# One projection product over the whole array, and row 0's uniform attention through one block and a row sum

## The chip, the cores and the metric

The kernel runs on one core of one Trainium2 chip, in fp32 throughout. The metric is the device time of the program in microseconds. The engines are named as in the profile: PE is TensorE's matmul stream and PEld its weight loads, DVE is VectorE, ACT is ScalarE, POOL is GpSimd, and SP is the engine that issues most of the plain DMAs.

## The reference

Eight sequences of 512 tokens with 256 features go through three residual steps:

```
x = x + 0.5 * moe(layernorm(x))          # f1
x = x + attention(layernorm(x))
x = x + 0.5 * moe(layernorm(x))          # f2

attention(x):                            # x: 8 x 512 x 256, already normalised
    sim   = x x^T / 16                   # only s < t counts
    A     = the 8 best s for each t (fewer where t < 8, none for t = 0)
    q, k  = x Wq^T, x Wk^T               # 32 features each
    score = q k^T / sqrt(32), and -1e9 where A is 0
    msg   = softmax(score) x
    return gelu(gain * (mix * x + (1 - mix) * msg) + bias) * scale
```

Row 0 of a sequence has no earlier token, so all its 512 scores are -1e9 and its softmax is uniform: its message is the mean over all 512 rows. Every other row has at least one chosen neighbour, and its weights outside the chosen ones are zero. The expert step (moe) sends each token to two of eight experts with 512 hidden features.

## The kernel before, in words

The tokens of a whole step are sorted into **tiles** of 256 slots, each for one expert. There are 39 tiles for f1, then 13 for f2 over the first five sequences (f2a) and 26 for the rest (f2b). A loop over all 78 tiles writes out the order of every engine's instructions by hand; nothing is reordered after that. For each tile it emits four times `up` (eight passes of 128x256 into `ph`, a silu on ACT, a product `g` on DVE), the transposes of the next tile's rows (`ptx`, copied to `xT` by DVE), two times `down` (eight passes each into `py`), and two times `put`: ACT scales `py` to `y`, and POOL issues an indirect DMA that adds the rows to `acc_d`. Between the two `put`s POOL issues the gather of a later tile's weights (`w`), after them the gathers of its rows (`xr`). fp32 products run as two passes per matmul instruction, transposes as one.

Between these pieces the loop calls `side()`, which advances a generator by one step: the attention of one sequence after another, and, where it is due, the routing of f2a and f2b. A sequence starts two tiles after its rows are complete, so that one sequence of attention falls into every four tiles of f1. Each engine works its instructions off in the order in which they were emitted; whatever waits holds up what is behind it on that engine.

One sequence of attention has these steps, a `side()` call each:

- layernorm on DVE (`xn`), then on POOL two operations over the whole sequence for `own`, the part of the output that doesn't depend on the neighbours;
- the transposes of `xn` into `xnT`;
- the queries, then the keys: a product of `wq_sb` and of `wk_sb` (128x32 each) with `xnT`, both into tiles called `pq`, copied by ACT into `q` and `k_`, 32 partitions each. In the loop the first stands between the two `down`s of a tile, the second after its `put`s;
- nine steps in which the four blocks c of 128 rows pass through a chain, one step apart: `similar` (`psim` on PE, `sim` on ACT, the mask of the diagonal block on POOL), `choose` (MAX8 and MATCH_REPLACE on DVE), `score` (`psc` on PE with 32 rows of the array, then `kept`, `hit`, `sc`, `nmax` on DVE), `exponential` (ACT), `turn` (transposes `pte` on PE, `exT` on DVE), `message` (`pm` on PE, `msg` and the sum into `own` on DVE). Block c works on columns 0 to (c+1)*128.

Block 0 holds row 0. In `exponential`, `turn` and `message` it is therefore worked over all 512 columns; the columns from 128 on are a constant -1e9, written once into two buffers `first`. Within a step the order is choose, exponential, message, turn, score, similar, each for its block.

All PSUM tiles of the attention and the routing come from one pool of three buffers in turn (`ps_a`), so a new product waits until the third product before it has been read. `ph` has three buffers of its own; `sim`, `hit`, `ex` and `exT` have two each in SBUF.

```
L573            for n, wn in enumerate((wq_sb, wk_sb)):
L576                    pq[:DH, :T], lhsT=wn[:, k, :], rhs=xnT[:, k, :], start=(k == 0), stop=(k == KD - 1)
L621            nc.tensor.matmul(psc[:, :W], lhsT=q[:, c * P : W], rhs=k_[:, :W], start=True, stop=True)
L642            W = T if c == 0 else (c + 1) * P
L671        for j in range(NC + len(steps) - 1):
L672            for lag in (1, 3, 5, 4, 2, 0):
```

Of the kernel before, what the change touches and what calls it, by code (L numbers as in the profile page):

```python
# [9 lines left out]
F32 = mybir.dt.float32  # L10
I32 = mybir.dt.int32
U32 = mybir.dt.uint32
AF = mybir.ActivationFunctionType
ALU = mybir.AluOpType
# [4 lines left out]
P = 128  # L19
# [7 lines left out]
def kernel(  # L27
# [13 lines left out]
    nc = tc.nc  # L41
    B, T, D = x.shape
    DH = wqT.shape[1]
    E = gwT.shape[1]
    KD = D // P
    FF = wexp.shape[1] // (3 * KD)
    KF = FF // P
    NC = T // P
# [17 lines left out]
    const = ctx.enter_context(tc.tile_pool(name="const", bufs=1))  # L66
    dram = ctx.enter_context(tc.tile_pool(name="dram", bufs=1, space=DRAM))
    wpool = ctx.enter_context(tc.tile_pool(name="wpool", bufs=3))
    work = ctx.enter_context(tc.tile_pool(name="work", bufs=2))
# [6 lines left out]
    ps_a = ctx.enter_context(tc.tile_pool(name="ps_a", bufs=3, space=PSUM))  # L76
# [34 lines left out]

    gw_sb = const.tile([P, KD, E], F32, tag="gw_sb", name="gw_sb")
    nc.scalar.dma_start(gw_sb, gwT.rearrange("(k p) e -> p k e", p=P))
    wq_sb = const.tile([P, KD, DH], F32, tag="wq_sb", name="wq_sb")
    nc.scalar.dma_start(wq_sb, wqT.rearrange("(k p) h -> p k h", p=P))
    wk_sb = const.tile([P, KD, DH], F32, tag="wk_sb", name="wk_sb")
    nc.scalar.dma_start(wk_sb, wkT.rearrange("(k p) h -> p k h", p=P))
    gain_sb = const.tile([P, D], F32, tag="gain_sb", name="gain_sb")
    nc.scalar.dma_start(gain_sb, gain.to_broadcast([P, D]))
    bias_sb = const.tile([P, D], F32, tag="bias_sb", name="bias_sb")  # L120
# [20 lines left out]
    scale = const.tile([P, 1], F32, tag="scale", name="scale")  # L141
# [3 lines left out]

    first = []
    for i in range(2):
        t = const.tile([P, T], F32, tag=f"first{i}", name=f"first{i}")
        nc.vector.memset(t[:, P:], MASKED)
        first.append(t)  # L150


    def layernorm(src, name):
# [28 lines left out]
    def transposed(xn, name):  # L182

        xnT = work.tile([P, KD, T], F32, tag="xnT", name=f"xnT_{name}")
        for k in range(KD):
            pt = ps_a.tile([P, 512], F32, tag="pa", name=f"pt_{name}_{k}")
            for c in range(NC):
                nc.tensor.transpose(pt[:, c * P : (c + 1) * P], xn[:, c, k * P : (k + 1) * P], ident)  # L188
            nc.scalar.copy(xnT[:, k, :], pt[:, :T])
        return xnT  # L190
# [369 lines left out]
    def attention(b, x1, tables):  # L560

        xn = yield from layernorm(x1, f"at_{b}")

        own = work.tile([P, NC, D], F32, tag="own", name=f"own_{b}")
        nc.gpsimd.tensor_mul(own, xn, mix_gain.unsqueeze(1).to_broadcast([P, NC, D]))
        nc.gpsimd.tensor_add(own, own, bias_sb.unsqueeze(1).to_broadcast([P, NC, D]))
        yield
        yield
        xnT = transposed(xn, f"at_{b}")
        yield  # L570
        qk = []
        for n, wn in enumerate((wq_sb, wk_sb)):
            pq = ps_a.tile([P, 512], F32, tag="pa", name=f"pq{n}_{b}")  # L573
            for k in range(KD):
                nc.tensor.matmul(  # L575
                    pq[:DH, :T], lhsT=wn[:, k, :], rhs=xnT[:, k, :], start=(k == 0), stop=(k == KD - 1)  # L576
                )
            t = work.tile([DH, T], F32, tag=f"qk{n}", name=f"qk{n}_{b}")
            nc.scalar.activation(t, pq[:DH, :T], AF.Copy, scale=1.0 / math.sqrt(DH) if n == 0 else 1.0)
            qk.append(t)  # L580
            yield
        q, k_ = qk
        sims, hits, scores, exs, exTs = {}, {}, {}, {}, {}

        def similar(c):

            W = (c + 1) * P
            rows = slice(c * P, W)
            psim = ps_a.tile([P, 512], F32, tag="pa", name=f"psim_{b}_{c}")
            for k in range(KD):  # L590
                nc.tensor.matmul(  # L591
                    psim[:, :W], lhsT=xnT[:, k, rows], rhs=xnT[:, k, :W], start=(k == 0), stop=(k == KD - 1)
                )
            sim = work.tile([P, T], F32, tag="sim", name=f"sim_{b}_{c}")
            nc.scalar.activation(sim[:, :W], psim[:, :W], AF.Copy, scale=1.0 / math.sqrt(D))
            nc.gpsimd.affine_select(
                out=sim[:, rows], in_=sim[:, rows], pattern=[[-1, P]], compare_op=ALU.is_gt, fill=NEG, base=0,
                channel_multiplier=1,
            )
            sims[c] = sim  # L600

        def choose(c):

            W, sim = (c + 1) * P, sims[c]
            top = small.tile([P, 8], F32, tag="top", name=f"top_{b}_{c}")
            nc.vector.max(top, sim[:, :W])
            hit = work.tile([P, T], F32, tag="hit", name=f"hit_{b}_{c}")
            nc.vector.match_replace(hit[:, :W], top, sim[:, :W], HIT)
            if c == 0:

                nc.gpsimd.affine_select(
                    out=hit[:, :P], in_=hit[:, :P], pattern=[[-1, P]], compare_op=ALU.is_gt, fill=0.0, base=0,
                    channel_multiplier=1,
                )
            hits[c] = hit

        def score(c):

            W, hit = (c + 1) * P, hits[c]
            psc = ps_a.tile([P, 512], F32, tag="pa", name=f"psc_{b}_{c}")  # L620
            nc.tensor.matmul(psc[:, :W], lhsT=q[:, c * P : W], rhs=k_[:, :W], start=True, stop=True)  # L621
            kept = work.tile([P, T], F32, tag="kept", name=f"kept_{b}_{c}")
            nc.vector.scalar_tensor_tensor(
                kept[:, :W], hit[:, :W], HIT, psc[:, :W], ALU.is_equal, ALU.mult
            )
            nc.vector.tensor_scalar(hit[:, :W], hit[:, :W], HIT, MASKED, ALU.is_lt, ALU.mult)
            sc = first[b % 2] if c == 0 else work.tile([P, W], F32, tag=f"sc{c}", name=f"sc_{b}_{c}")
            nc.vector.tensor_add(sc[:, :W], kept[:, :W], hit[:, :W])
            nmax = small.tile([P, 1], F32, tag=f"nmax{c}", name=f"nmax_{b}_{c}")
            nc.vector.tensor_reduce(nmax, sc[:, :W], AX.X, ALU.max, negate=True)  # L630
            scores[c] = sc, nmax

        def exponential(c):
            W = T if c == 0 else (c + 1) * P
            sc, nmax = scores[c]
            ex = work.tile([P, T], F32, tag="ex", name=f"ex_{b}_{c}")
            tot = small.tile([P, 1], F32, tag=f"tot{c}", name=f"tot_{b}_{c}")
            nc.scalar.activation(ex[:, :W], sc[:, :W], AF.Exp, bias=nmax, accum_out=tot)
            exs[c] = ex, tot

        def turn(c):
            W = T if c == 0 else (c + 1) * P  # L642
            pt = ps_a.tile([P, 512], F32, tag="pa", name=f"pte_{b}_{c}")
            for s in range(W // P):
                nc.tensor.transpose(pt[:, s * P : (s + 1) * P], exs[c][0][:, s * P : (s + 1) * P], ident)
            exT = work.tile([P, T], F32, tag="exT", name=f"exT_{b}_{c}")
            nc.vector.tensor_scalar(exT[:, :W], pt[:, :W], 0.0, None, ALU.max)
            exTs[c] = exT

        def message(c):  # L650
            W = T if c == 0 else (c + 1) * P
            pm = ps_a.tile([P, 512], F32, tag="pa", name=f"pm_{b}_{c}")
            for s in range(W // P):
                nc.tensor.matmul(  # L654
                    pm[:, :D],
                    lhsT=exTs[c][:, s * P : (s + 1) * P],
                    rhs=xn[:, s, :],
                    start=(s == 0),
                    stop=(s == W // P - 1),
                )  # L660

            part = small.tile([P, 1], F32, tag="part", name=f"part_{b}_{c}")
            nc.vector.reciprocal(part, exs[c][1])
            nc.vector.tensor_scalar(part, part, 0.0, rest, ALU.max, ALU.mult)
            msg = work.tile([P, D], F32, tag="msg", name=f"msg_{b}_{c}")
            nc.vector.scalar_tensor_tensor(msg, pm[:, :D], part, gain_sb, ALU.mult, ALU.mult)
            nc.vector.tensor_add(own[:, c, :], own[:, c, :], msg)


        steps = (similar, choose, score, exponential, turn, message)  # L670
        for j in range(NC + len(steps) - 1):  # L671
            for lag in (1, 3, 5, 4, 2, 0):  # L672
                if 0 <= j - lag < NC:
                    steps[lag](j - lag)
            yield

        nc.scalar.activation(own, own, AF.Gelu)
        yield
        nc.vector.scalar_tensor_tensor(x1, own, scale, x1, ALU.mult, ALU.add)
        yield  # L680
        yield from ffn_begin(b, x1, "f2", tables)
# [161 lines left out]
```

## Time and profile before

| | |
|---|---|
| time, three runs | 1261.3 us median (1258.34, 1261.3, 1262.29) |
| the profiled execution | 1258.32 us; span 1256.6 us, TensorE clock 0.98 |
| PE, PEld busy | 1159.4 us, 955.8 us |
| DVE, ACT, POOL busy | 573.7 us, 343.6 us, 532.8 us |
| DMA | 195.30 MB, 155 GB/s |
| pq matmuls (L575) | 64 passes of 128x512, 592 ns median each |
| psc matmuls (L621) | 64 passes, 270 to 692 ns |
| POOL on own (L565, L566) | 8 x 2355 ns and 8 x 2345 ns |

[...] passes that follow each other start closer together than their durations. The start-to-start distance is therefore what a group costs on PE. A number in brackets behind a row of the trace is the idle time of that engine ahead of the instruction and what ended it. The span runs roughly like this: set-up and routing of f1 until 116 us, expert tiles alone until about 260, attention between the tiles until 840, the routing of f2b beside tiles of f2a until 945, and tiles alone to the end.

### The profile page before, as it was taken

The page shows a single profiled execution, that of the slowest core. Times are in us where ns is not written, and L with a number is a line of the kernel's source. Part 1 is how long each engine was busy: PE and PEld are TensorE (multiplying, and loading weights), DVE is VectorE, ACT ScalarE, POOL GpSimd, SP SyncE. Part 2 cuts the span into 40 slices and gives each one's busy share as a digit, 9 for nine tenths or more (in the row PEclk, how much of TensorE's full clock was granted, in tenths as well). Part 3 has the DMA queues.
Part 4 walks back from the last instruction along what each step waited for, and adds up shares of the span by engine and source line. Part 5 has one row for each costly group of instructions (what it writes and reads, how often), then busy time and mean ns, then how long its engine had stood idle before and what let it go on. Part 6 is the DMA issues. An engine that isn't in the chain of part 4 may idle for free.

```text
span 1256.6 us, 14941 instructions
## 1 busy us (share of the span) xinstructions
PE 1159.4 (92%) x5470; PEld 955.8 (76%) x5470; DVE 573.7 (46%) x1713; ACT 343.6 (27%) x718; POOL 532.8 (42%) x464
## 2 busy tenths in 40 slices
PE   5854999989999999999799999998999999999996
PEld 4743888867768676777668778687888888888885
DVE  7484221226555564736768465567732222221221
ACT  2200122224343343424323243342122222222221
POOL 0002355553443435352522544534345555554553
PEclk9997999989999999999999999999999999999998
DMA  8402566654645346363622645344456776677664
GB/s 296 150 1 112 183 182 182 188 155 129 184 114 152 121 137 181 86 197 103 184 68 67 185 134 175 91 154 134 135 138 197 201 201 187 183 215 233 190 198 91
DMA packets 69337, 195.30 MB, mean 155 GB/s; under 512 B 8336, under 2 KB 54160, under 8 KB 59152
## 3 DMA queue, kind: packets, MB, share of 16 engines
q0 software_dynamic: 41184, 163.60, 45.3%
q1 hardware_dynamic: 25600, 29.36, 7.0%
q10 hardware_dynamic: 2480, 1.39, 0.4%
q8 instruction: 43, 0.70, 0.2%
q14 instruction: 30, 0.25, 0.1%
HBM read 156.05 MB, written 42.47 MB: 158 GB/s over the span
## 4 chain that ended last, share of the span: by engine, by line
PE 63%; DVE 15%; issue 11%; DMA 4%; ACT 4%; POOL 1%; POOLq 0%; ACTq 0%; DVEq 0%
PE ph_f L522 14%; PE ph_f2b L522 11%; PE py_f L537 9%; PE py_f2b L537 6%; PE ph_f2a L522 4%; PE py_f2a L537 3%; PE psim L591 3%; PE pm L654 2%; PE pq L575 2%; DMA acc_d_f<-y_f2b,tokens_f2b 2%; DMA xr_f2b<-xn_d_f,tokens_f2b 1%; PE psc L621 1%; PE pt_at L188 1%; PE pg_f L217 1%; PE pl_f2b L369 1%
## 5 line engine op out<-in xcount | busy, mean ns | idle before, releaser
L522 PE MATMUL ph_f<-xT_f,w_f 128*128 128x256 f32 x1248 | 289.0, 384 | 0.8 <-DVE xT_f L514 0.8
L522 PEld LDWEIGHTS ph_f<-xT_f,w_f 128*128 128x128 f32 x1248 | 235.7, 192 | 44.7 <-issue 11.2
L549 POOL DMA_INDIRECT acc_d_f<-y_f,tokens_f x78 | 125.5, 1609 | 261.8 <-ACT y_f L548 223.5
L522 PE MATMUL ph_f2b<-xT_f2b,w_f2b 128*128 128x256 f32 x832 | 183.8, 379 | 0.0
L531 DVE TENSOR_TENSOR g_f<-silu_f,ph_f 128x256 f32<-128x256 f32 x156 | 64.3, 418 | 258.9 <-ACT silu_f L530 257.0
L522 PEld LDWEIGHTS ph_f2b<-xT_f2b,w_f2b 128*128 128x128 f32 x832 | 158.1, 190 | 21.5
L537 PE MATMUL py_f<-w_f,g_f 128*128 128x256 f32 x624 | 148.8, 389 | 0.0
L531 DVE TENSOR_TENSOR g_f2b<-silu_f2b,ph_f2b 128x256 f32<-128x256 f32 x104 | 43.8, 421 | 223.8 <-ACT silu_f2b L530 223.8
L537 PEld LDWEIGHTS py_f<-w_f,g_f 128*128 128x128 f32 x624 | 117.1, 194 | 27.1 <-issue 13.0
L549 POOL DMA_INDIRECT acc_d_f<-y_f2b,tokens_f2b x52 | 83.2, 1601 | 109.3 <-DMA acc_d_f<-y_f2b,tokens_f2b 56.0
L530 ACT ACTIVATE silu_f<-ph_f 128x256 f32<-128x256 f32 x156 | 59.7, 383 | 224.6 <-PE ph_f L522 209.8
L537 PE MATMUL py_f2b<-w_f2b,g_f2b 128*128 128x256 f32 x416 | 95.6, 383 | 0.0
L522 PE MATMUL ph_f2a<-xT_f2a,w_f2a 128*128 128x256 f32 x416 | 95.1, 380 | 0.0
L479 POOL DMA_INDIRECT w_f<-in_wexp,wrow_f x39 | 38.5, 987 | 123.2 <-DVE wrow_f L475 111.6
L479 POOL DMA_INDIRECT xr_f<-xn_d_f,tokens_f x78 | 76.6, 982 | 23.8 <-issue 23.8
L522 PEld LDWEIGHTS ph_f2a<-xT_f2a,w_f2a 128*128 128x128 f32 x416 | 77.7, 190 | 11.6 <-issue 1.6
L537 PEld LDWEIGHTS py_f2b<-w_f2b,g_f2b 128*128 128x128 f32 x416 | 78.2, 193 | 9.9
L549 POOL DMA_INDIRECT acc_d_f<-y_f2a,tokens_f2a x26 | 41.9, 1613 | 93.0 <-ACT y_f2a L548 89.1
L530 ACT ACTIVATE silu_f2b<-ph_f2b 128x256 f32<-128x256 f32 x104 | 39.9, 383 | 127.8 <-PE ph_f2b L522 126.5
L548 ACT ACTIVATE y_f<-py_f,wslot_f 128x256 f32<-128x256 f32 x78 | 32.7, 470 | 103.4 <-PE py_f L537 103.4
L479 POOL DMA_INDIRECT xr_f2b<-xn_d_f,tokens_f2b x52 | 50.4, 968 | 15.8 <-issue 15.8
L531 DVE TENSOR_TENSOR g_f2a<-silu_f2a,ph_f2a 128x256 f32<-128x256 f32 x52 | 21.5, 418 | 72.3 <-ACT silu_f2a L530 72.2
(349 smaller groups left out, 1545.5 us busy)
## 6 DMA issues: line engine op xcount, KB each, us to landing
xn_d_f<-xn_f SPq DMA_DIRECT2D x16, 512.0 KB
xin<-in_x SPq DMA_DIRECT2D x8, 512.0 KB
acc_d_f<-xin SPq DMA_DIRECT2D x8, 512.0 KB
x<-acc_d_f SPq DMA_DIRECT2D x8, 512.0 KB
acc_d_f<-x SPq DMA_DIRECT2D x8, 512.0 KB
out<-acc_d_f SPq DMA_DIRECT2D x8, 512.0 KB
xr_f<-xn_d_f,tokens_f POOLq DMA_INDIRECT x78
acc_d_f<-y_f,tokens_f POOLq DMA_INDIRECT x78
```

The costliest lines, as they stand in the source:

```text
L188: nc.tensor.transpose(pt[:, c * P : (c + 1) * P], xn[:, c, k * P : (k + 1) * P], ident)
L217: nc.tensor.matmul(pg[:, c, :], lhsT=xnT[:, k, c * P : (c + 1) * P], rhs=gw_sb[:, k, :], start=(k == 0), stop=(k == KD - 1),)
L479: nc.gpsimd.indirect_dma_start(out=dst, out_offset=None, in_=table, in_offset=bass.IndirectOffsetOnAxis(ap=index.bitcast(U32), axis=0),)
L522: nc.tensor.matmul(ph[:, n, :], lhsT=wn[:, k, f * P : (f + 1) * P], rhs=self.xT[:, k, :], start=(k == 0), stop=(k == KD - 1),)
L530: nc.scalar.activation(s, ph[:, 0, :], AF.Silu)
L531: nc.vector.tensor_mul(self.g[:, f, :], s, ph[:, 1, :])
L537: nc.tensor.matmul(self.py[:, h, :], lhsT=self.g[:, f, h * P : (h + 1) * P], rhs=self.w2[:, f, :], start=(f == 0), stop=(f == KF - 1),)
L548: nc.scalar.activation(y, self.py[:, h, :], AF.Copy, scale=wslot[:, h, self.i : self.i + 1])
L549: add = nc.gpsimd.indirect_dma_start(out=self.acc_d, out_offset=bass.IndirectOffsetOnAxis(ap=tokens[:, h, self.i : self.i + 1].bitcast(U32 ...
L575: nc.tensor.matmul(pq[:DH, :T], lhsT=wn[:, k, :], rhs=xnT[:, k, :], start=(k == 0), stop=(k == KD - 1))
L591: nc.tensor.matmul(psim[:, :W], lhsT=xnT[:, k, rows], rhs=xnT[:, k, :W], start=(k == 0), stop=(k == KD - 1))
L654: nc.tensor.matmul(pm[:, :D], lhsT=exTs[c][:, s * P : (s + 1) * P], rhs=xn[:, s, :], start=(s == 0), stop=(s == W // P - 1),)
```

## The change

One weight tile `wkq_sb` of 128 columns holds the key weights, the query weights, and both again; one product with it replaces the two. ACT copies all 128 rows of the result to `kq` (keys in rows 0 to 31), and after the next step rows 32 to 63, scaled, to rows 0 to 31 of one of two buffers `queries`, whose other rows were set to zero once. The scores are then products over 128 rows, in which the zero rows of `queries` cancel the rest of `kq`.

For row 0, block 0 keeps two blocks of columns instead of four. Its second block is -1e9 throughout; in `message` that block is multiplied with `after`, the sum of the row blocks 1, 2 and 3 of `xn`, which POOL makes with two additions. The sum of the weights, which ACT formed over 256 columns, is raised by 256 times one weight of the second block.

The change of `W` stands in `exponential`, `turn` and `message`, the two lines on `tot` in `turn`, the choice of `after` in `message`:

```diff
-    wq_sb = const.tile([P, KD, DH], F32, tag="wq_sb", name="wq_sb")
-    nc.scalar.dma_start(wq_sb, wqT.rearrange("(k p) h -> p k h", p=P))
-    wk_sb = const.tile([P, KD, DH], F32, tag="wk_sb", name="wk_sb")
-    nc.scalar.dma_start(wk_sb, wkT.rearrange("(k p) h -> p k h", p=P))
+    wkq_sb = const.tile([P, KD, P // DH, DH], F32, tag="wkq_sb", name="wkq_sb")
+    for n in range(P // DH):
+        nc.scalar.dma_start(wkq_sb[:, :, n, :], (wqT if n % 2 else wkT).rearrange("(k p) h -> p k h", p=P))
...
-        t = const.tile([P, T], F32, tag=f"first{i}", name=f"first{i}")
+        t = const.tile([P, 2 * P], F32, tag=f"first{i}", name=f"first{i}")
         nc.vector.memset(t[:, P:], MASKED)
         first.append(t)
+    queries = []
+    for i in range(2):
+        t = const.tile([P, T], F32, tag=f"queries{i}", name=f"queries{i}")
+        nc.vector.memset(t, 0.0)
+        queries.append(t)
...
-        qk = []
-        for n, wn in enumerate((wq_sb, wk_sb)):
-            pq = ps_a.tile([P, 512], F32, tag="pa", name=f"pq{n}_{b}")
-            for k in range(KD):
-                nc.tensor.matmul(
-                    pq[:DH, :T], lhsT=wn[:, k, :], rhs=xnT[:, k, :], start=(k == 0), stop=(k == KD - 1)
-                )
-            t = work.tile([DH, T], F32, tag=f"qk{n}", name=f"qk{n}_{b}")
-            nc.scalar.activation(t, pq[:DH, :T], AF.Copy, scale=1.0 / math.sqrt(DH) if n == 0 else 1.0)
-            qk.append(t)
-            yield
-        q, k_ = qk
+        pq = ps_a.tile([P, 512], F32, tag="pa", name=f"pq_{b}")
+        for k in range(KD):
+            nc.tensor.matmul(
+                pq[:, :T], lhsT=wkq_sb[:, k].rearrange("p n h -> p (n h)"), rhs=xnT[:, k, :], start=(k == 0),
+                stop=(k == KD - 1),
+            )
+        kq = work.tile([P, T], F32, tag="kq", name=f"kq_{b}")
+        nc.scalar.copy(kq, pq[:, :T])
+        yield
+        q = queries[b % 2]
+        nc.scalar.activation(q[:DH], pq[DH : 2 * DH, :T], AF.Copy, scale=1.0 / math.sqrt(DH))
+        after = work.tile([P, D], F32, tag="after", name=f"after_{b}")
+        nc.gpsimd.tensor_add(after, xn[:, 1, :], xn[:, 2, :])
+        for c in range(3, NC):
+            nc.gpsimd.tensor_add(after, after, xn[:, c, :])
+        yield
...
-            nc.tensor.matmul(psc[:, :W], lhsT=q[:, c * P : W], rhs=k_[:, :W], start=True, stop=True)
+            nc.tensor.matmul(psc[:, :W], lhsT=q[:, c * P : W], rhs=kq[:, :W], start=True, stop=True)
...
-            W = T if c == 0 else (c + 1) * P
+            W = max(c + 1, 2) * P
...
+            if c == 0:
+                ex, tot = exs[c]
+                nc.vector.scalar_tensor_tensor(tot, ex[:, P : P + 1], float(T - 2 * P), tot, ALU.mult, ALU.add)
...
-                    rhs=xn[:, s, :],
+                    rhs=after if c == 0 and s == 1 else xn[:, s, :],
```

More of the change, by code (lines that the diff above doesn't have):

```diff
@@ L641, in turn @@
         def turn(c):
-            W = T if c == 0 else (c + 1) * P
+            W = max(c + 1, 2) * P
+            if c == 0:
+                ex, tot = exs[c]
+                nc.vector.scalar_tensor_tensor(tot, ex[:, P : P + 1], float(T - 2 * P), tot, ALU.mult, ALU.add)
             pt = ps_a.tile([P, 512], F32, tag="pa", name=f"pte_{b}_{c}")
@@ L650, in message @@
         def message(c):
-            W = T if c == 0 else (c + 1) * P
+            W = max(c + 1, 2) * P
             pm = ps_a.tile([P, 512], F32, tag="pa", name=f"pm_{b}_{c}")
```

## The prediction

> **What bounds the kernel now.** I read the page first (shares, slices, chain), then the busy time by stretches, then TensorE's waits, and then the instructions of one sequence in order of time, engine by engine.
>
> ```profile
> PE 1159.4 (92%) x5470; PEld 955.8 (76%) x5470; DVE 573.7 (46%) x1713; ACT 343.6 (27%) x718; POOL 532.8 (42%) x464
> ...
> 470.00:540.00 70.00, 68.18 (x313) 52.12 (x312) 38.48 (x117) 26.32 (x50) 30.97 (x27) 1.00 0.49 143
> 945.00:1122.00 177.00, 177.00 (x855) 155.93 (x854) 37.59 (x82) 38.44 (x98) 98.80 (x82) 1.00 0.67 193
> ```
>
> The columns of the last two rows are the stretch, its length, busy us of PE, PEld, DVE, ACT and POOL, clock, DMA share, GB/s. PE is the bound, in the attention stretch too: 470 to 540 holds one sequence, and PE is idle for 1.8 us of it. PE's waits there are three, 1.0 on xn, 0.4 on f2's xn, 0.4 on exT. The first queries' matmuls of sequences 1 to 4 start at 344.57, 414.50, 484.44, 554.36: a period of 69.93 us. Sequence 3, on PE and then on POOL and DVE:
>
> ```profile
> 484.37 1.90 PE L575 MATMUL pq<-xnT_at,wq_sb 128*32 128x512 f32 x4
> 486.20 1.99 PE L537 MATMUL py_f<-w_f,g_f 128*128 128x256 f32 x8
> 488.13 1.90 PE L575 MATMUL pq<-xnT_at,wk_sb 128*32 128x512 f32 x4
> 489.96 1.99 PE L522 MATMUL ph_f<-xT_f,w_f 128*128 128x256 f32 x8
> ...
> 496.65 0.48 PE L621 MATMUL psc<-qk,qk 32*128 32x128 f32 x2
> 497.06 1.56 PE L591 MATMUL psim<-xnT_at 128*128 128x384 f32 x4
> 498.45 1.89 PE L522 MATMUL ph_f<-xT_f,w_f 128*128 128x256 f32 x8
> ...
> 508.08 1.89 PE L654 MATMUL pm<-xn_at,exT 128*128 128x256 f32 x8
> 509.81 0.38 PE L645 MATMUL pte<-ident,ex 128*128 128x128 f32 x2
> ```
> ```profile
> 495.41 0.96 POOL L479 DMA_INDIRECT xr_f<-xn_d_f,tokens_f  x1 [0.30 <-issue]
> 496.39 0.30 POOL L596 TENSOR_SCALAR_AFFINE_SELECT sim<-sim 128x128 f32<-128x128 f32 x1
> ```
> ```profile
> 496.72 0.29 DVE L606 MAX8 top<-sim 128x8 f32<-128x128 f32 x1 [1.72 <-POOL sim L596]
> 500.86 0.42 DVE L531 TENSOR_TENSOR g_f<-silu_f,ph_f 128x256 f32<-128x256 f32 x1 [0.76 <-ACT silu_f L530]
> 510.01 0.48 DVE L666 SCALAR_TENSOR_TENSOR msg<-pm,part,gain_sb 128x256 f32<-128x256 f32 x1 [1.09 <-PE pm L654]
> ```
>
> A group of matmuls costs the time to the next group's start: eight 128x256 passes take 1.73 us (508.08 to 509.81), but 1.93 between the two pq groups. The second lesson is on POOL: the mask of block 0's similarities starts 0.02 us after the row gather ahead of it, although ACT had written sim at 492.78, and DVE's MAX8 waits 1.72 us for it. So the choice of neighbours starts when POOL's queue lets it, not when PE does.
>
> **What the Trainium skill says.** "TensorEngine Tiling (Array Packing)", Key Properties: a change of tiling mode drains TensorE. The trace agrees: 0.09 to 0.11 us are lost before and again after each pq (32 columns) and psc (32 rows) group. "TensorE: Matmul & The Clock Gate", Why this matters: a product over 32 rows takes the time of one over 128. The trace differs: two 384-column passes of psc take 0.84 us (505.41 to 506.25), 0.64 at psim's spacing.
>
> **The change, part by part** (per sequence, full-array spacing from psim and pm: 0.43, 0.32, 0.216, 0.108 us a pass of 512, 384, 256, 128 columns).
>
> 1. One product for queries and keys. From the py group ahead of pq to the ph group behind the second, PE takes 482.55 to 491.79 = 9.24 us; with one full-width pq it is 3 x 1.73 + 4 x 0.43 = 6.91. Gain 2.33, of which 0.3 falls before the first y and 2.03 after it.
> 2. Scores over 128 rows. psc with its neighbours, against full spacing: block 0 (1.82 + 0.41 + 1.39) - (1.73 + 0.22 + 1.28) = 0.39; the other three likewise 0.40, 0.40, 0.38. Gain 1.57. Weight loads go from 182 to 190 ns, beside other passes.
> 3. Row 0's block: two transposes instead of four, 0.22, and four passes instead of eight, 1.73 - 0.86 = 0.87.
>
> PE's work falls by 4.99 us a sequence, 39.9 in all. But PE can keep only what DVE's chain gives.
>
> 4. ACT: two copies before and after (586 ns each, the full-width one priced by the 128x512 copy, 588); exp of block 0 falls from 722 to 508. ACT has gaps of 1 us and more there; nothing.
> 5. POOL: two dependent adds of 128x256, in its queue behind the two row gathers and ahead of the mask of block 0. No such row exists. A quarter of own's 128x1024 (2355 ns) gives 0.59 each; with the 4497 ns for 2048 elements that the skill's "GPSIMD Engine Reference", Elementwise, states, a line through both gives 0.72. I take 0.66, with 0.10 of gaps 1.42 us; bounds 1.25 and 1.55. Were they free, the mask would come 0.3 earlier than now, because y does. Queued behind them are the five masks; the next y comes 11 us later.
> 6. DVE: exT of block 0 from 682 to 418, plus one 128x1 multiply-add (0.2, less overlap): -0.15.
>
> Now DVE's chain. The mask moves by -0.31 + 1.42 = +1.11, and MAX8 to 497.83. All to nmax of block 0 (500.10) moves with it. There DVE now waits 0.76 (0.84 with the overlap) for the fourth silu. ACT writes that after the similarities of block 2, which reuse block 0's buffer and so wait for its MATCH_REPLACE (ends 497.41 + 1.11 = 498.52); with copy and silu (0.49, 0.38) it is ready at 499.4, before nmax ends at 501.21. So g starts 0.27 late, not 1.11. Part 6 makes it 0.12. Then the wait of 1.09 for pm goes: pm is ready at 507.8, DVE at 509.06, so msg starts 0.95 earlier than now. From there exT, kept, nmax, the exp with its two table loads, silu and g follow each other without a gap as now, so pm of blocks 2 and 3 and all behind moves by 0.95.
>
> PE meets this as waits. kept of block 0 (ends 500.30) frees the PSUM buffer of psim 3 (three buffers in turn), for which PE is ready at 498.29: py ends at 487.72, then ph, psim, ph, psim, ph, psc, psim, ph, the transposes of the next tile and psc take 1.73, 0.43, 1.73, 0.86, 1.73, 0.22, 1.28, 1.73, 0.43, 0.43. Wait: 2.07. exT of block 0 (ends 506.69, PE ready at 506.40): 0.35. exT of block 2 (516.05 - 0.95 = 515.10), PE ready at 513.33 (pm 507.61, then 0.22, 0.86, 1.73, 0.86, 0.32, 1.73): 1.83, where 0.18 is lost now. 4.99 - 4.07 = 0.92, the same by the other road. Eight sequences: **-7.6 us**. The sequence that shares DVE with f2a's routing (633 to 700) has its MAX8 at 646.95 without a wait; the mask would come at about 646.8, then the same two waits fall away: about the same gain.
>
> 7. Set-up: two more weight DMAs (0.55 us of issue each, 32 KB) in ACT's queue, and fillings of 1.3 instead of 0.76 us while DVE waits 2.46 us for x. DMA is 0.90 to 0.95 busy until 40 us: +0.5, bounds 0 and +2. If that cover is gone they cost 1.1.
>
> The routing, the expert stages before 260 and the tail with its DMA waits after 1122 are untouched. The profiled execution took 1258.3 us (span 1256.6 plus 1.7 around it), 3.0 below the median of 1261.3; I apply -7.1 to the median: **1254 us**.
>
> **Rivals.**
> - Adds off the path: POOL has slack after all (the select's start is rough), or DVE's chain does not feel the mask. Then the chain gains 0.95 + 1.42 = 2.37 a sequence: -19, 1242. Against it: gather and mask touch (496.37, 496.39). Chance 0.10. All 39.9 us, 1221, needs a DVE chain that nowhere binds, which its 2.2 us of waits in 13 us don't allow: 0.03.
> - Adds dear, no change. Break-even is 1.42 + 0.95 = 2.37 us for both, 1.14 each. The masks run at 2.3 ns an element with no visible fixed part, but take up to 0.77 instead of 0.29 where DVE runs beside them; DVE is idle at 497. About 1261; 0.15.
> - **Slower: the clock.** The new waits lie in bursts of 2 us. The clock page's Part 1 has half rate follow a 3.4 us window of little activity. The trace shows how little is enough: a wait of 1.71 at 664.4, and then
>
> ```profile
> 663.90:667.40 3.50, 1.79 (x7) 0.72 (x6) 2.86 (x10) 1.73 (x3) 2.69 (x3) 1.00 0.74 129
> 667.40:670.80 3.40, 3.40 (x10) 2.66 (x10) 2.37 (x4) 0.00 (x0) 2.17 (x2) 0.50 0.96 369
> ```
> eight ph passes in 3.53 us, 1.8 more. After the wait for psim 3 a later wait would absorb it; after pm of block 2 it lies on the path. Place: behind pm of block 2; price 1.8 a sequence; it decides from 4 of 8 sequences (7.1 / 1.8). All eight: +14 - 7 = 1268. Against it: the window above also held narrow psc and transposes, whereas 2 us of idle leave 1.4 us of full matmuls, and a window with 0.97 idle and transposes (479.4 to 482.8, PE busy 2.43) kept full clock. 0.12.
>
> **Numbers.** Forecast 0.60, rivals 0.13, 0.15, 0.12. A measurement of this kernel tells about 0.3% (3.8 us) from no change. Faster: 0.59 of the forecast and 0.13 = 0.72; same: 0.15 and 0.01; slower 0.12. The forecast's own range, from the adds' bounds and set-up, is 1251 to 1257; to 1242 and 1261 it takes in the free and the dear adds.
>
> **What would show it.** pq four passes at 0.43 with no loss around; psc passes at 0.108 to 0.43; adds of 0.6 to 0.7 us; MAX8 of block 0 waiting 5 us for POOL; PE waiting some 2 us for kept at psim and 2 for exT at pm; msg of block 0 without its wait for pm; a period of 69.0. If the period is under 68, the adds or the chain are looser than I say; a clock of 0.5 inside the sequences is the slower rival; adds above 1.1 us the dear one.

## The result, and the profile after

The changed kernel takes **1257.17 us** (median of 12 runs, 1252.93 to 1262.07), the kernel before, measured beside it, 1262.34 (12 runs, 1256.14 to 1266.87). The ratio is 0.9957, 95% interval 0.9942 to 0.9973: 5.2 us or 0.43% faster, with 7.1 forecast. The profiled execution took 1255.58 us, its span 1253.9.

The page first: engines' busy time and the shares of the chain that ended last, after the change; under them the chain's shares before it.

```profile
PE 1127.1 (90%) x5390; PEld 951.1 (76%) x5390; DVE 571.7 (46%) x1723; ACT 341.4 (27%) x718; POOL 544.5 (43%) x480
...
PE 44%; DVE 21%; issue 16%; POOL 9%; DMA 6%; ACT 4%; POOLq 0%; DVEq 0%; ACTq 0%
```
```profile
PE 63%; DVE 15%; issue 11%; DMA 4%; ACT 4%; POOL 1%; POOLq 0%; ACTq 0%; DVEq 0%
```

PE's busy time is 32 us shorter, and POOL's share of the chain went from 1% to 9%. The two stretches that the prediction shows of the kernel before:

```profile
470.00:540.00 70.00, 64.75 (x307) 52.05 (x306) 38.18 (x118) 26.28 (x51) 33.08 (x30) 1.00 0.50 147
945.00:1122.00 177.00, 177.00 (x854) 155.86 (x853) 37.42 (x82) 39.05 (x99) 98.52 (x81) 1.00 0.67 193
```

Between 470 and 540 PE is now idle for 5.25 us instead of 1.8; the expert tiles behind 945 are as they were. One sequence begins with each `own` on POOL; these starts of sequences 1 to 4 are 340.59, 409.63, 478.68, 547.74: a period of **69.05 us** for 69.93. Sequence 3 on PE (instructions in order of time; the bracket is PE's idle time ahead and what ended it):

```profile
479.25 1.89 PE L543 MATMUL py_f<-w_f,g_f 128*128 128x256 f32 x8
480.98 1.88 PE L579 MATMUL pq<-xnT_at,wkq_sb 128*128 128x512 f32 x4
482.70 1.89 PE L543 MATMUL py_f<-w_f,g_f 128*128 128x256 f32 x8
484.42 1.89 PE L528 MATMUL ph_f<-xT_f,w_f 128*128 128x256 f32 x8
486.15 0.61 PE L602 MATMUL psim<-xnT_at 128*128 128x128 f32 x4
...
494.59 0.60 PE L632 MATMUL psc<-kq,queries 128*128 128x256 f32 x2
495.94 1.98 PE L602 MATMUL psim<-xnT_at 128*128 128x512 f32 x4 [0.76 <-ACT sim L606]
...
503.44 0.70 PE L669 MATMUL pm<-xn_at,exT 128*128 128x256 f32 x2 [1.19 <-DVE exT L662]
503.98 0.59 PE L669 MATMUL pm<-after,exT 128*128 128x256 f32 x2
504.41 0.38 PE L660 MATMUL pte<-ident,ex 128*128 128x128 f32 x2
...
511.94 1.56 PE L669 MATMUL pm<-xn_at,exT 128*128 128x256 f32 x6 [1.49 <-DVE exT L662]
```

The first four groups follow each other at 1.72 to 1.73 us, pq among them: here PE's work did shrink as worked out. Three waits, 3.44 us together, take most of the saving back; the kernel before had none over 0.2 us in these places. What stands behind them is POOL's queue, shown with DVE's first step of block 0 and ACT's copy of block 2:

```profile
491.80 0.96 POOL L485 DMA_INDIRECT xr_f<-xn_d_f,tokens_f  x1 [0.30 <-issue]
492.79 0.73 POOL L590 TENSOR_TENSOR after<-xn_at 128x256 f32<-128x256 f32 x1
493.60 0.72 POOL L592 TENSOR_TENSOR after<-after,xn_at 128x256 f32<-128x256 f32 x1
494.28 0.29 POOL L607 TENSOR_SCALAR_AFFINE_SELECT sim<-sim 128x128 f32<-128x128 f32 x1
```
```profile
494.60 0.30 DVE L617 MAX8 top<-sim 128x8 f32<-128x128 f32 x1 [5.24 <-POOL sim L607]
...
505.92 0.48 DVE L681 SCALAR_TENSOR_TENSOR msg<-pm,part,gain_sb 128x256 f32<-128x256 f32 x1
```
```profile
495.40 0.49 ACT L606 ACTIVATE sim<-psim 128x384 f32<-128x384 f32 x1 [3.90 <-DVE hit L619]
```

ACT had block 0's similarities ready at 487.14 (486.86 and 0.28). Their mask starts 7.1 us later, when the row gathers and the two additions are through. MAX8 waits 5.24 us for it instead of 1.72; ACT waits for the sim buffer that block 0's MATCH_REPLACE leaves, and PE for ACT. msg of block 0, DVE's second row, no longer waits for pm.

### The profile page after: what moved, and what is told of

The parts are those of the page before. It is cut to its first block, busy times and chain, and to the rows that moved or that the text cites. A ratio compares the mean times of both kernels' runs of the same rounds, so it can differ in the third digit from the quotient of the medians.

```text
span 1253.9 us, 14804 instructions
## 1 busy us (share of the span) xinstructions
PE 1127.1 (90%) x5390; PEld 951.1 (76%) x5390; DVE 571.7 (46%) x1723; ACT 341.4 (27%) x718; POOL 544.5 (43%) x480
## 4 chain that ended last, share of the span: by engine, by line
PE 44%; DVE 21%; issue 16%; POOL 9%; DMA 6%; ACT 4%; POOLq 0%; DVEq 0%; ACTq 0%
PE ph_f2b L528 10%; PE ph_f L528 10%; PE py_f2b L543 5%; PE py_f L543 5%; PE ph_f2a L528 4%; DMA acc_d_f<-y_f2b,tokens_f2b 3%; PE py_f2a L543 2%; POOL acc_d_f L555 2%; POOL own L571 2%; POOL own L572 1%; PE pm L669 1%; DMA xr_f2b<-xn_d_f,tokens_f2b 1%; DVE hit L619 1%; DVE nmax L641 1%; PE pl_f2b L375 1%
## 5 line engine op out<-in xcount | busy, mean ns | idle before, releaser
L669 PE MATMUL pm<-xn_at,exT 128*128 128x256 f32 x160 | 42.8, 398 | 22.4 <-DVE exT L662 22.4
```

The costliest lines, as they stand in the source:

```text
L669: nc.tensor.matmul(pm[:, :D], lhsT=exTs[c][:, s * P : (s + 1) * P], rhs=after if c == 0 and s == 1 else xn[:, s, :], start=(s == 0), stop= ...
```

## The experiments

The theory: a sequence's length is set by the mask of block 0 behind POOL's gathers and by DVE's chain from there, so the saving counts only as far as that chain shortens. The rival that most runs are set against: PE's work counts, and the new waits are something else. Each row: median time, ratio to the kernel before with its 95% interval, the regular period, and the time of seven sequences from the first `own` to the last. The kernel before was measured again beside each group of runs, hence its three medians between 1262.3 and 1263.5; each ratio is to the one of its own group.

| kernel | us | ratio | period | seven sequences |
|---|---|---|---|---|
| before | 1262.3 to 1263.5 | | 69.93 | 515.4 |
| changed | 1257.2 | 0.9957 (0.9942 to 0.9973) | 69.05 | 508.6 |
| e1 adds early | 1244.5 | 0.9874 (0.985 to 0.9897) | 67.73 | 499.0 |
| e2 projection only | 1243.8 | 0.9857 (0.9835 to 0.9879) | 67.73 | 498.1 |
| e3 row 0 only | 1258.8 | 0.9988 (0.997 to 1.0006) | 69.57 | 513.0 |
| e4 adds twice | 1268.4 | 1.0059 (1.0038 to 1.008) | 70.6 | 517.7 |
| e5 scores on 32 rows | 1258.7 | 0.9958 (0.9939 to 0.9978) | 69.00 | 508.1 |
| e6 masks off POOL | 1238.9 | 0.9795 (0.9772 to 0.9817) | 66.88 | 492.2 |
| e7 before, masks off POOL | 1271.2 | 1.0054 (1.0035 to 1.0073) | 70.81 | 517.6 |

### e1: the additions where POOL is idle

```diff
         nc.gpsimd.tensor_add(own, own, bias_sb.unsqueeze(1).to_broadcast([P, NC, D]))
+        after = work.tile([P, D], F32, tag="after", name=f"after_{b}")
+        nc.gpsimd.tensor_add(after, xn[:, 1, :], xn[:, 2, :])
+        for c in range(3, NC):
+            nc.gpsimd.tensor_add(after, after, xn[:, c, :])
...
-        after = work.tile([P, D], F32, tag="after", name=f"after_{b}")
-        nc.gpsimd.tensor_add(after, xn[:, 1, :], xn[:, 2, :])
-        for c in range(3, NC):
-            nc.gpsimd.tensor_add(after, after, xn[:, c, :])
```

> The changed kernel, with the two POOL additions emitted right behind the two operations on own, where POOL waited 1.92 us for y in the changed kernel, instead of behind the row gathers. Theory (POOL's queue delays the mask of block 0, the mask starts DVE's chain, and the chain sets the period of a sequence): the mask comes 1.5 us earlier, the period falls from 69.05 to 67.5 us, the time by 12 us against the changed kernel and 17 against the kernel before. Rival (PE's new waits come from PSUM buffers and ACT's copies, or from DVE's own work, whatever POOL does): the period stays at 69.0 and the time stands 5 us below the kernel before.

The same instructions on every engine, in another place of one queue, give a period of 67.73. POOL of this run, in order of time:

```profile
481.47 0.73 POOL L574 TENSOR_TENSOR after<-xn_at 128x256 f32<-128x256 f32 x1
482.28 0.73 POOL L576 TENSOR_TENSOR after<-after,xn_at 128x256 f32<-128x256 f32 x1
483.43 1.63 POOL L555 DMA_INDIRECT acc_d_f<-y_f,tokens_f  x1 [0.42 <-ACT y_f L554]
...
489.86 0.96 POOL L485 DMA_INDIRECT xr_f<-xn_d_f,tokens_f  x1 [0.30 <-issue]
490.84 0.30 POOL L607 TENSOR_SCALAR_AFFINE_SELECT sim<-sim 128x128 f32<-128x128 f32 x1
```

The additions lie in the gap ahead of the first scatter, which is still 0.42 long behind them; the mask follows the gather with no gap, as before the change. PE's wait at psim is gone, and the one for exT of block 2 is 1.7 us long. So of the 1.50 us by which the additions hold the mask back in the changed kernel, 1.32 went into each regular sequence's length, from this one place.

### e2 and e3: one part without the other

e2 is the changed kernel with row 0 over 512 columns again and without the additions; e3 is the kernel before with row 0's part alone, the additions behind the gathers.

```diff
 e2
-        after = work.tile([P, D], F32, tag="after", name=f"after_{b}")
-        nc.gpsimd.tensor_add(after, xn[:, 1, :], xn[:, 2, :])
-        for c in range(3, NC):
-            nc.gpsimd.tensor_add(after, after, xn[:, c, :])
...
-            W = max(c + 1, 2) * P
+            W = T if c == 0 else (c + 1) * P
 e3
+            if n == 1:
+                after = work.tile([P, D], F32, tag="after", name=f"after_{b}")
+                nc.gpsimd.tensor_add(after, xn[:, 1, :], xn[:, 2, :])
+                for c in range(3, NC):
+                    nc.gpsimd.tensor_add(after, after, xn[:, c, :])
...
-            W = T if c == 0 else (c + 1) * P
+            W = max(c + 1, 2) * P
```

> Only the one product for queries and keys and the scores over 128 rows; row 0 is worked over all 512 columns as in the kernel before, and there are no additions on POOL. Theory: PE's work falls by 3.9 us a sequence, y comes 0.3 us earlier and with it the mask; DVE then doesn't wait for the fourth silu and for pm of block 0 any more, 2.2 us a sequence: period 67.7, time 17 us below the kernel before, thus less time than the whole change although PE has more to do. Rival (what counts is PE's work): the whole change, with 4.99 us less work, is the faster one, and this one gains at most 3.9/4.99 of its 5 us, 4 us.

> Only row 0's part: block 0 over two blocks of columns, with the sum of the row blocks on POOL behind the row gathers; queries and keys by two products and scores over 32 rows as in the kernel before. Theory: PE's work falls by 1.09 us a sequence, but the mask comes 1.5 us later and takes up DVE's two waits: between 0 and 0.6 us a sequence are left, period 69.3 to 69.9, time 0 to 5 us below the kernel before. Rival (PE's work counts): period 68.8, 9 us below.

e2 does more work on PE than the whole change (1.09 us a sequence by the prediction's sum) and is 13.4 us faster: the rival can't give that sign. Its period equals e1's, so with the additions off the path row 0's smaller products are worth nothing that the period shows. e3 gains 0.36 a sequence, and its time is within what can be told from no change. The two parts alone give -2.20 and -0.36, together -0.88: they don't add, because the second part's additions lengthen the chain that sets the first part's gain (e1 and e2, without that delay, both have 67.73).

### e4: the additions twice

```diff
             nc.gpsimd.tensor_add(after, after, xn[:, c, :])
+        nc.gpsimd.tensor_add(after, xn[:, 1, :], xn[:, 2, :])
+        for c in range(3, NC):
+            nc.gpsimd.tensor_add(after, after, xn[:, c, :])
```

> The changed kernel with the two POOL additions done twice, at the same place (same result). Theory: the mask comes 1.5 us later still, nothing behind it takes that up: period 70.5, time 12 us above the changed kernel, some 7 us above the kernel before. Rival (POOL's queue isn't what PE waits for): period 69.0, time as the changed kernel's, 5 us below the kernel before.

The period grows by 1.55 us for 1.6 us more of additions, with MAX8 waiting 6.83 us: from here the price on the path is one for one. The time from gather to mask is now 3.1 us, 0.7 over the break-even of 2.37 that the prediction gives for the additions, and the period is 0.7 above that of before. This run also shows what the prediction's clock rival speaks of. PE's row at psim 3 of sequence 1, the same row of sequence 2, and the stretch around the first:

```profile
361.68 3.40 PE L605 MATMUL psim<-xnT_at 128*128 128x512 f32 x4 [2.33 <-ACT sim L609]
...
432.27 1.99 PE L605 MATMUL psim<-xnT_at 128*128 128x512 f32 x4 [2.37 <-ACT sim L609]
```
```profile
362.10:365.50 3.40, 3.40 (x6) 1.55 (x5) 3.24 (x11) 2.03 (x4) 0.00 (x0) 0.50 0.00 0
```

After 2.33 us of waiting the clock is halved for 3.4 us; after 2.37 us in the next sequence it is not. Of seven waits of 2.33 to 2.37 us in this place three were followed by half clock (at 361.68, 573.57 and 737.03) and four were not (at 291.03, 432.27, 502.93 and 807.62), so the length of the wait alone doesn't decide. The sequence with the window shown took 70.56 us and the next, which had none, 70.67: PE's later waits absorb it. In the changed kernel no wait of a regular sequence is longer than 1.5 us, and the clock stayed full from 273 to 617.

### e5: the scores on 32 rows again

```diff
-            nc.tensor.matmul(psc[:, :W], lhsT=q[:, c * P : W], rhs=kq[:, :W], start=True, stop=True)
+            nc.tensor.matmul(psc[:, :W], lhsT=q[:DH, c * P : W], rhs=kq[:DH, :W], start=True, stop=True)
```

> The changed kernel with the scores' product on 32 rows again (part 2 undone; the one product and row 0's part stay). TensorE then has 1.57 us a sequence more to do. Theory (in the changed kernel TensorE isn't the bound; the block masks on GpSimd's queue are, and TensorE waits 3.4 us a sequence for the weights and for the copy of the similarities): the 1.57 us fall into those waits, the MAX8 waits for the mask stay at 5.2 and 0.3 us, the period stays 69.05 to 69.5 us and the time is within 3 us of the changed kernel's, about 1257 to 1261. Rival (TensorE's work counts in full): period 70.6, time about 1270, above the kernel before.

The second of the change's three savings is undone, 1.57 us a sequence by the prediction's sum, and no loss is seen: ratio 0.9958 for 0.9957, period 69.00 for 69.05. PE of this run:

```profile
496.42 0.69 PE L632 MATMUL psc<-kq,queries 32*128 32x256 f32 x2
497.30 1.98 PE L602 MATMUL psim<-xnT_at 128*128 128x512 f32 x4 [0.18 <-ACT sim L606]
...
504.80 0.70 PE L669 MATMUL pm<-xn_at,exT 128*128 128x256 f32 x2 [0.81 <-DVE exT L662]
...
513.22 1.56 PE L669 MATMUL pm<-xn_at,exT 128*128 128x256 f32 x6 [1.18 <-DVE exT L662]
```

The three waits are 2.17 instead of 3.44 us: 1.27 of the 1.57 us of work lie where PE would have waited; where the other 0.30 went is open. MAX8 waits 5.25 for the mask, as in the changed kernel.

### e6 and e7: the masks off POOL's queue

Both take the masks of the similarities away from POOL: one more product adds -1e30 on and above the diagonal, and the hits of block 0 are multiplied on DVE. e6 starts from e1 (with one buffer for `after`), e7 from the kernel before (with one for `msg`), to make room.

```diff
+    never = const.tile([P, P], F32, tag="never", name="never")
+    nc.gpsimd.affine_select(
+        out=never, in_=zeros[:, :P], pattern=[[-1, P]], compare_op=ALU.is_gt, fill=-1.0e30, base=0, channel_multiplier=1
+    )
...
+            nc.tensor.matmul(psim[:, rows], lhsT=ident, rhs=never, start=False, stop=True)
...
-            nc.gpsimd.affine_select(
-                out=sim[:, rows], in_=sim[:, rows], pattern=[[-1, P]], compare_op=ALU.is_gt, fill=NEG, base=0,
-                channel_multiplier=1,
-            )
...
-                nc.gpsimd.affine_select(
-                    out=hit[:, :P], in_=hit[:, :P], pattern=[[-1, P]], compare_op=ALU.is_gt, fill=0.0, base=0,
-                    channel_multiplier=1,
-                )
+                nc.vector.tensor_mul(hit[:, :P], hit[:, :P], earlier)
```

> The changed kernel with the two additions right behind own's two operations, and with the block masks taken off GpSimd: the diagonal block's mask is added to psim by one more product (identity times a constant with -1e30 on and above the diagonal, 128 columns for each block, about 0.86 us of TensorE a sequence by the passes of pt_f), and the hits of block 0 are masked by a product with a constant on VectorE. Theory (the masks behind GpSimd's queue set the sequence): MAX8 has no wait for GpSimd left, TensorE is the bound again, and the period is 69.93 - 4.99 + 0.86 plus some waits for exT of up to 1 us, 65.8 to 66.8, time 1228 to 1238. Rival (after the adds are moved, another chain sets the sequence, VectorE's own work or the weights' copies): period stays at 67.5 to 67.7 as in the run with the early adds, time about 1243 to 1246.

> The same removal of the masks from GpSimd, on the kernel before, nothing else of the change. Theory (before, TensorE's work was the bound with 0.4 us of waits for exT a sequence, and the masks were just hidden): the product adds 0.86 us a sequence and takes away at most 0.4 + 0.8 us (the waits for exT and behind silu), so the period is 69.7 to 70.8, time 1260 to 1270. Rival (the masks were the bound already before the change): period falls to about 68.5, time about 1250.

e6 has the shortest time of all, 1238.9 us, 2.05% under the kernel before, though PE does 0.86 us more a sequence. Its period of 66.88 is just above the range given, its time 0.9 us above; e7, with 70.81 and 1271.2, is as little above its own. DVE and then PE of e6:

```profile
486.03 0.29 DVE L621 MAX8 top<-sim 128x8 f32<-128x128 f32 x1
```
```profile
439.44 1.56 PE L670 MATMUL pm<-xn_at,exT 128*128 128x256 f32 x6 [1.08 <-DVE exT L663]
```

MAX8 starts without a wait for POOL; of the three waits of the changed kernel one, for exT of block 2, is left. And two of e7's PE waits in three sequences, summed (engine, line, releaser: us, times, longest); the kernel before has 2.9 and 1.2 there:

```profile
PE pt_at L197 <- DVE xn_at L186: 2.9, 3, 1.0
PE pm L655 <- DVE exT L648: 1.3, 3, 0.4
```

On the kernel before, the same edit costs 0.88 a sequence, which is the added product's 0.86: there PE had no wait to put it in. So in its regular sequences the kernel before was bound by PE, with the mask just hidden; the changed one is bound by the mask. The pair also prices the change with that queue out of the way (and the additions early): 70.81 - 66.88 = 3.93 of the 4.99 us, where the change as made got 0.88. The missing 1.06 is about the size of e6's wait for exT of block 2, 1.08; that it is this wait was not tested.

### e8: the set-up

The four loads of `wkq_sb` stand behind `scale_in` in ACT's queue instead of ahead of `gain_sb`.

```diff
     nc.scalar.dma_start(scale_in, log_scale.to_broadcast([P, 1]))
+    for n in range(P // DH):
+        nc.scalar.dma_start(wkq_sb[:, :, n, :], (wqT if n % 2 else wkT).rearrange("(k p) h -> p k h", p=P))
```

> The changed kernel with the two halves' four weight loads behind scale_in in ScalarE's queue; a look at the set-up alone. Theory (scale_in landed later because two more loads stand ahead of it, and VectorE waits 3.1 us for it at sp_abs): sp_abs waits 1.6 us or less, and the first transposition starts 1 to 1.5 us sooner, at 122.5 to 123.0 instead of 124.0 us. Rival (the late start is the two memsets of queries on VectorE, 0.5 us each): the first transposition stays at 123.5 to 124.2.

One run, 1258.39 us. The first transposition of rows starts at 122.50 instead of 124.03, at the time expected, but not for the reason given. sp_abs on DVE, in the changed kernel and then in e8:

```profile
11.54 0.16 DVE L136 SCALAR_TENSOR_TENSOR sp_abs<-scale_in 128x1 f32<-128x1 f32 x1 [3.14 <-DMA scale_in<-in_log_scale]
```
```profile
9.35 0.16 DVE L136 SCALAR_TENSOR_TENSOR sp_abs<-scale_in 128x1 f32<-128x1 f32 x1 [2.96 <-DMA scale_in<-in_log_scale]
```

It comes 2.2 us sooner and still waits 2.96, where 1.6 or less was expected. At the routing's end (L401, 109.13 and 108.68) only 0.45 of that is left. Another 1.05 of the 1.53 us comes from the clock: it is halved from 112.5 us in the changed kernel and from 114.1 in e8, and DVE waits 2.51 and 1.46 us for PE's routing product `po_f` there. All seven profiled kernels with the changed set-up reach L401's step between 108.5 and 109.4 us, e8 among them; the kernel before, e3 and e7 reach it between 107.4 and 107.7. So the set-up costs about 1 to 2 us up to there; whether the loads or the memsets cost it stays open. The first `own` starts at 270.25 and 270.22: nothing of what e8 gained reaches the sequences in these two executions.

## Why the prediction was right or wrong, point by point

- **Parts 1 to 3, PE's work: right.** py, pq, py, ph take 479.25 to 486.15, 6.90 us (6.91 worked out). The four psc groups keep 0.22, 0.43, 0.65 and 0.86 us. Of row 0's block, two transposes take 0.22 and four passes 0.97, which is 0.86 and a restart after a wait. No loss is seen at pq's or psc's edges (ph ahead of the first psc takes 1.72), as the Trainium skill's "TensorEngine Tiling (Array Packing)", Key Properties, would have it with no change of mode.
- **Part 5, the additions: a term mis-sized, by little.** They take 0.73 and 0.72, not 0.66; from gather to mask it is 1.50 with the gaps (491.80 + 0.96 = 492.76, mask 494.28, less the 0.02 of before), for 1.42, within its bounds. The higher end, by the price in the Trainium skill's "GPSIMD Engine Reference", Elementwise, was the better one. The prediction's sum for it is off, though: the line through that 4497 ns and own's 2345 to 2355 gives an estimate of 0.73 to 0.75, not 0.72.
- **The shift along DVE: right in kind, close in size.** Counted from `own` (481.97 before, 478.68 after): MAX8 of block 0 comes 1.17 later (+1.11 said), the fourth g 0.32 later without its old wait of 0.76 (+0.27 said, +0.12 with part 6), msg of block 0 0.80 sooner without its wait for pm (0.95 said). The period fell by 0.88, for 0.92 by PE's road and 0.95 by DVE's.
- **PE's waits: the sum about right, the places not.** Waits of 2.07, 0.35 and 1.83, together 4.25, were forecast at psim 3, pm of block 0 and pm of block 2 (the times given there differ by 2.01, 0.29 and 1.77; 0.06 each was added unsaid). The trace's brackets have 0.76, 1.19 and 1.49. Counted from start to start they are 0.92 (494.59 + 0.43 to 495.94), 1.35 and 1.66, and each restart loses about 0.1 more, together 4.2.
- **The buffer of psim 3.** The step of the forecast that failed is "kept of block 0 frees the PSUM buffer of psim 3 (three buffers in turn)": the product started at 495.94, before kept of block 0 (496.79), so it did not take that buffer, and the account of the three buffers in turn does not hold here. It waits for ACT's copy of block 2, which ended at 495.89. In the kernel before, e3 and e7, which have two products for queries and keys, the same instruction waits for a semaphore of DVE. In the regular sequences of the changed kernel and of e1, e2, e4, e5 and e8, which have one, it waits for one of ACT (in e6 for DVE's again). So the change moved this wait itself; by what rule the buffers are handed out, the runs don't show. That copy waited 3.90 for block 0's MATCH_REPLACE, so the cause is still the late mask. The error left the total alone: exT of block 2 lies behind all of them on the one chain, and what PE doesn't wait at psim it waits later.
- **"About the same gain" in the sequence with f2a's routing: not seen, and open.** From 619.54 to 709.77 it took 90.23 us, before 90.35. PE's waits there grew by 3.0 us, the one for msg of block 0 at psc from 1.7 to 3.2, so that most of what PE saved became waiting, which would fit DVE's routing work setting this stretch. How much of the time is lost to that is not settled, because the clock blurs it: between 612 and 672 it was halved for 17.0 us, before for 13.6, in e8 for 10.2, and e8's stretch, of the same instructions as the changed kernel's, took 88.00.
- **Part 7, the set-up: +1.5 us at the first transposition, +0.5 said, bounds 0 to 2.** At the first `own` it is +0.75 (269.47 and 270.22). But e1, e4 and e5, with the same set-up as the changed kernel, reach it at 271.1 to 271.6, and e3, with the weights loaded as before, at 271.6: at the first `own` the cost is smaller than the scatter (e8, above, has what it is at the routing's end).
- **The ends were taken as quiet; in a single execution they are not, and part of the total is luck.** From the last `own` to the end before took 471.7 us and after 475.1, with nothing changed there; the other kernels have 470.7 to 479.2. Of the 6.8 us that the seven sequences gained, the first distance alone has 2.26 (72.63 to 70.37), where 0.88 is regular: the clock was halved around its start for 6.8 us before and for 3.4 after, and in e8, with 6.8, it is 71.27. That the sum comes near to seven times the forecast 0.95 is thus in part chance. And of these 6.8 us the two profiled spans show 2.7 at the end, with 0.75 gone at the start and 3.4 lost in the tail; the medians show 5.2, and their interval (0.9942 is -7.3 us) still holds the forecast's -7.1.
- **Rivals.** Free additions: no as the change stands, but e1 gives what they would: 1244.5, where 1242 was said. Dear additions: 0.73 is far from the break-even of 1.14; e4, which reaches 3.1 us for them, is slower than before, as that break-even has it. The clock: not in the regular sequences of the changed kernel; in e4 it does halve, and costs nothing visible. Its price was read a little too high: the eight ph passes take 3.40 us from start to start (667.17 to 670.57), not 3.53, so 1.7 more. The Trainium skill's "TensorE: Matmul & The Clock Gate", Part 1, has half rate follow an idle window of about 3.4 us, and calls this window free-running. Here 2.33 to 2.35 us of wait were enough three times of seven. A free-running window would let equal waits end differently, but no run here tests that.

## What to carry to other kernels

When PE's busy time falls, ask which chain on the slower engines comes next and how much room there is to it: here 2.2 us of 5 (e2), and two small additions in the wrong place of POOL's queue took 1.3 of them. A place for new work is chosen by what is queued behind it: the same two instructions cost nothing in the gap ahead of a scatter that waits anyway. And when a short operation sits behind DMA issues in a queue (a 0.3 us mask, 7.1 us after its input), moving it to the engine with most work can still pay: PE's 0.86 us bought 0.85 of period on top of e1, and only after PE had been relieved; before, it cost 0.88.

## What the runs showed of the hardware that was not expected

- A 128x256 addition on POOL takes 0.72 to 0.73 us, a 128x1024 one 2.35: with four times the elements 3.2 times as long. A straight line through the two sizes leaves a fixed part of about 0.18 us, an estimate.
- The length of a single PE wait doesn't tell whether half clock follows: of seven waits of 2.33 to 2.37 us in e4, three were followed by 3.4 us of half clock and four were not. Seven of 1.69 to 1.71 us in e1 were not, though one of 1.71 us in the kernel before was (the prediction shows it).
- After each of the three new waits PE lost about 0.1 us more than the wait itself: the two passes of 256 columns behind the wait of 1.19 start 0.54 us ahead of the next group, the following two 0.43 (503.44, 503.98 and 504.41 in the profile after).
